# A new order of all engines for a two-branch cross-attention, with 9 score groups read from PSUM and 13 row by row

## The chip, the cores and the metric

The kernel runs on one core of a Trainium2 chip. A core has five engines with instruction queues of their own: TensorE (PE in the profile, with PEld for its weight loads), VectorE (DVE), ScalarE (ACT), GpSimd (POOL) and SyncE (SP), which here issues nearly all DMAs. The metric is the device time of one execution in microseconds. Before the change it was 500.68 us, the median of 3 runs (498.34 to 501.45).

## The reference

The inputs are tokens x (2 x 2048 x 640), a context (2 x 154 x 1024), six weight matrices and a bias, all float32. There are 20 heads of 32 channels. The first 77 context tokens are text, the other 77 an image prompt with key and value weights of its own; each half has its own softmax, and the two results are added.

```
q    = heads(x @ Wq.T)
k,v  = heads(text @ Wk.T), heads(text @ Wv.T)
k',v' = heads(ip @ Wk_ip.T), heads(ip @ Wv_ip.T)
out  = softmax(q k^T / sqrt(32)) v + softmax(q k'^T / sqrt(32)) v'
y    = merge_heads(out) @ Wo.T + bo + x
```

## The kernel before

All matrices lie with the contracted dimension first, so the 640 channels are five chunks of 128, and a chunk holds four heads. The work on one batch and one chunk is a pair; there are 10 pairs (batch 0 first). A pair's 2048 tokens are two units of 1024, so there are 20 units u = 0 to 19. A unit has two halves of 512 tokens (h) and three score groups (s) of 3, 3 and 2 blocks of 128 tokens; a group has 4 heads x 2 softmaxes for each block, so 24, 24 and 16 softmax rows of 77 keys on each partition.

The order of the whole program is written out by hand in `SCHEDULE` (from L560), a list of words that `emit` turns into instructions one after the other. Each engine executes its own instructions in that order; semaphores make it wait for data of the others. A word is a letter for the step, the unit or pair, and after the @ the PSUM bank or half of PSUM (8 banks, two halves of 4). The words that matter below:

- `q.u.h` the query product on TensorE (L199, five matmuls of 512 columns), `cq.u.h` its scaled copy out of PSUM on ScalarE (L209); `k.c.t` and `v.c.t` the key and value products (L140), `ck` and `cv` their copies.
- `Rs.u` the scores of group s on TensorE (L231: four heads side by side, 12 or 8 blocks in all). `Ks.u` copies them to the SBUF tile pb on ScalarE (L243), `Ms.u` takes the row maxima on VectorE (L279, or L282 from PSUM), `Ss.u` subtracts them on GpSimd (L293), `Es.u` is the exponential on ScalarE (one instruction, L299), `Ds.u` the row sums on VectorE (L304), `Is.u` their reciprocal (L309), `Ns.u` the normalising product on GpSimd (L314), `Ts.u` a transposition of 32 x 32 blocks on VectorE (L321).
- Three sets choose another way for a group (u, s). In DIRECT nothing is copied: the maxima and the exponentials read PSUM. In DIRECT and BIASED the exponential is one ScalarE instruction for each row, with the maximum as its bias (L267), and the subtraction on GpSimd falls away. In SUMMED, ScalarE adds up each row as well, and the sum on VectorE falls away. Groups of BIASED are first copied to SBUF.
- `A.q` the attention product of pair q on TensorE (L330: 80 matmuls in 32 x 32 tiles, 320 instructions with the weight loads), `CA.q` its copy out of PSUM. `SQ.c` and `VS.p.half` bring the values into the layout that it needs: a transposition on VectorE (L150), then eight small DMAs on SyncE (L156) for each VS.
- `LX.u.h` loads a block of 512 tokens of batch 1 (1280 KB, L184), `LQ.p` query weights (320 KB, L190), `LK.n` key or value weights (512 KB, L130), `LO` the output weights (1600 KB, L162, into the room of the context). `SF.i.part` fetches tokens to which the output is added (256 KB, L459 and L457), `SS.i.part` stores finished output (L465, L463). All of these stand in SyncE's one queue. The DMAs take eight semaphores in turn, so SyncE waits for an earlier DMA on the same semaphore before it issues the next on it.
- `m1` to `m7` with `.i` are the seven products of a Strassen-like scheme for the output projection of batch 0 (L488, L498), `cm` adds them to the output on VectorE (L513, L519); m3 joins the bank of m5 and so waits for cm5, as m6, m7 and m4 follow m1, m6 and m7. `G` and `W` are sums on GpSimd for it, `o` and `co` its last chunk (L469, L479). The output projection of batch 1 is a similar scheme with 33 products: `V` and `X` form sums of weights and tokens on VectorE (ending d) or GpSimd (ending p) at L826 and L832, `F` are the products (L846), `Y` the additions (L790, L792), each followed by a store (L796) once a block is finished.

[...] Outside the set-up all engine work is placed by the words above; nothing is placed by a scheduler.

Of the kernel before, what the change touches and what calls it, by code (L numbers as in the profile page):

```python
# [9 lines left out]
F32 = mybir.dt.float32  # L10
# [10 lines left out]
def kernel(  # L21
# [43 lines left out]
        (11, 0), (12, 0), (13, 0), (13, 2), (14, 0), (14, 2), (15, 1), (15, 2), (16, 2), (18, 1),  # L65
    }
    BIASED = {
        (3, 2), (4, 0), (5, 2), (6, 2), (8, 2), (9, 2), (10, 2), (11, 2), (12, 2), (18, 2), (19, 2),
    }
    SUMMED = {  # L70
        (10, 2), (12, 0), (12, 2), (13, 0), (13, 2), (14, 0), (15, 1), (16, 2), (18, 1), (18, 2), (19, 2),
# [480 lines left out]
    for t in range(2):  # L552
# [216 lines left out]
    for c, stages in enumerate(chains_of):  # L769
        for _, text in stages:  # L770
            for _, t in terms(text):
                for h in range(NH):
                    o = int(t[0]), NH * int(t[1]) + h
# [115 lines left out]
```

## Time and profile before

| | |
|---|---|
| median of 3 runs | 500.68 us (498.34 to 501.45) |
| profiled execution | 503.08 us, its span 501.3 us |
| TensorE busy | 492.2 us, 4114 passes |
| TensorE weight loads busy | 290.7 us, 4114 |
| VectorE busy | 410.7 us |
| ScalarE busy | 306.8 us |
| GpSimd busy | 376.5 us |
| granted TensorE clock over the span | 0.997 |
| DMA | 69.38 MB, mean 138 GB/s |

A page of the profile has the busy time of each engine, the span in 40 equal slices, the chain of work that ended last, and groups of instructions by line: operation, what is written from what, count, then busy time, mean of one in ns, and the idle time before them with what ended it. A row of the waits says which engine and line waited for whom: us in total, times, longest. A row of the timeline has start and duration in us, and in brackets the idle time before it. A row of the windows has the stretch, its length, then busy time and number of instructions of PE, PEld, DVE, ACT and POOL, then the granted TensorE clock, the DMA share and GB/s. In a row of the DMA view stand a queue, its packets, MB, and the share of the DMA engines' time; the queue of kind "instruction" numbered 8 brings TensorE's own program in packets of 16 KB. "Issue" is idle time in which an engine waited for nothing that the profile shows.

### The profile page before, as it was taken

The numbers are of one execution on the slowest core, as the hardware profiler recorded it, in microseconds if no ns is written. First come the engines' busy times: TensorE is split into PE (matmuls) and PEld (weight loads), VectorE is DVE, ScalarE is ACT, GpSimd is POOL, SyncE is SP. The second block draws the span as 40 slices with busy tenths as digits, with TensorE's granted clock in tenths as the row PEclk, the third lists the DMA queues.
The fourth block names the chain that finished last, engine by engine and source line by source line (L and its number), as shares of the span: only waits on it lengthen the run. The fifth ranks groups of instructions, "written<-read, shape, count | busy, mean of one in ns | idle before, by whom it ended". The sixth has DMA issues, their size and how long they took to land.

```text
span 501.3 us, 10439 instructions
## 1 busy us (share of the span) xinstructions
PE 492.2 (98%) x4114; PEld 290.7 (58%) x4114; DVE 410.7 (82%) x409; ACT 306.8 (61%) x970; POOL 376.5 (75%) x166
## 2 busy tenths in 40 slices
PE   9999999999999989999999999999999999999997
PEld 5665757567557547446646655665655685444442
DVE  0069989989999986978996888678799889998875
ACT  1175768798786866757999877485677955100000
POOL 0079998779898895968876748665889889799850
PEclk9999999999999998999999999999999999999999
DMA  8975403243044490748416337628442203320125
GB/s 264 356 209 151 133 3 100 54 119 84 23 112 150 150 288 19 248 133 330 134 54 229 94 119 274 222 87 264 144 158 90 86 1 106 127 84 1 43 101 192
DMA packets 67473, 69.38 MB, mean 138 GB/s; under 512 B 5472, under 2 KB 47200, under 8 KB 67424
## 3 DMA queue, kind: packets, MB, share of 16 engines
q1 hardware_dynamic: 66704, 68.00, 43.0%
q8 instruction: 32, 0.52, 0.4%
q10 hardware_dynamic: 720, 0.72, 0.4%
q14 instruction: 17, 0.14, 0.1%
HBM read 54.94 MB, written 10.49 MB: 131 GB/s over the span
## 4 chain that ended last, share of the span: by engine, by line
PE 90%; DMA 6%; SPq 2%; issue 1%; DVE 0%; ACT 0%
PE bank L199 30%; PE bank L846 11%; PE bank L488 10%; PE bank L231 10%; PE bank L330 10%; PE bank L140 9%; PE bank L469 7%; PE bank L498 3%; DMA x<-in_x_dram 2%; DMA aT<-in_L_xattn_Wk_ip_dram 2%; DMA wq<-in_L_xattn_Wq_dram 1%; DMA wo_ct<-in_L_xattn_Wo_dram 1%; SPq L156 1%; SPq L532 1%; SPq L130 0%
## 5 line engine op out<-in xcount | busy, mean ns | idle before, releaser
L314 POOL TENSOR_TENSOR pb<-pb,rden 128x1848 f32<-128x1848 f32 (+1 forms) x60 | 176.0, 2942 | 39.2 <-DVE rden L309 35.1
L199 PE MATMUL bank<-x,wq 128*128 128x512 f32 x400 | 180.0, 600 | 0.1
L293 POOL TENSOR_TENSOR pb<-pb,mx 128x1848 f32<-128x1848 f32 (+1 forms) x39 | 121.7, 3129 | 60.4 <-DVE mx L279 55.3
L199 PEld LDWEIGHTS bank<-x,wq 128*128 128x128 f32 x400 | 74.5, 191 | 85.9 <-issue 82.3
L321 DVE STREAM_TRANSPOSE pb<-pb 128x1920 f32<-128x1920 f32 (+1 forms) x60 | 115.8, 1934 | 6.3 <-POOL pb L314 5.9
L279 DVE TENSOR_REDUCE mx<-pb 128x24 f32<-128x1848 f32 (+1 forms) x50 | 91.4, 1843 | 31.6 <-ACT pb L243 31.5
L243 ACT COPY pb<-bank 128x462 f32<-128x462 f32 (+1 forms) x200 | 85.3, 540 | 42.2 <-PE bank L231 41.8
L304 DVE TENSOR_REDUCE den<-pb 128x24 f32<-128x1848 f32 (+1 forms) x49 | 91.5, 1878 | 15.6 <-ACT pb L299 11.9
L299 ACT ACTIVATE pb<-pb 128x1848 f32<-128x1848 f32 (+1 forms) x39 | 65.4, 1680 | 17.2 <-POOL pb L293 17.0
L267 ACT ACTIVATE pb<-bank,mx 128x77 f32<-128x77 f32 x208 | 59.1, 390 | 12.3 <-DVE mx L282 12.2
L231 PEld LDWEIGHTS bank<-kT,qT 32*128 32x128 f32 x1280 | 45.8, 184 | 29.7 <-issue 20.3
L231 PE MATMUL bank<-kT,qT 32*128 32x154 f32 x1280 | 57.0, 306 | 3.3 <-issue 2.6
L330 PE MATMUL bank<-pb,v 32*32 32x512 f32 x1600 | 55.2, 597 | 0.0
L267 ACT ACTIVATE pb<-pb,mx 128x77 f32<-128x77 f32 x184 | 52.7, 357 | 1.1 <-DVE mx L279 0.8
L140 PE MATMUL bank<-wo_ct,aT 128*128 128x154 f32 x320 | 46.9, 302 | 0.2 <-DMA aT<-in_L_xattn_Wk_ip_dram 0.2
L140 PEld LDWEIGHTS bank<-wo_ct,aT 128*128 128x128 f32 x320 | 44.4, 194 | 3.4 <-issue 2.8
L330 PEld LDWEIGHTS bank<-pb,v 32*32 32x32 f32 x1600 | 30.4, 103 | 21.7 <-issue 9.6
L267 ACT ACTIVATION_READ_ACCUMULATOR pb<-bank,mx 128x1 f32 x152 | 40.2, 273 | 0.0
L469 PE MATMUL bank<-aT,wo_ct 128*128 128x512 f32 x80 | 36.4, 596 | 0.0
L209 ACT ACTIVATE qT<-bank 128x512 f32<-128x512 f32 x40 | 24.3, 613 | 19.4 <-PE bank L199 19.3
L488 PE MATMUL bank<-aT,wo_ct 128*128 128x256 f32 x128 | 32.5, 386 | 0.6 <-DMA wo_ct<-in_L_xattn_Wo_dram 0.6
L488 PEld LDWEIGHTS bank<-aT,wo_ct 128*128 128x128 f32 x128 | 23.6, 190 | 8.3 <-issue 4.0
(75 smaller groups left out, 435.8 us busy)
## 6 DMA issues: line engine op xcount, KB each, us to landing
x<-in_x_dram SPq DMA_DIRECT2D x20, 1280.0 KB, 7.1
out_dram<-acc SPq DMA_DIRECT2D x20, 256.0 KB, 2.3
x<-in_x_dram SPq DMA_DIRECT2D x18, 256.0 KB, 5.4
acc<-in_x_dram SPq DMA_DIRECT2D x16, 256.0 KB, 3.7
out_dram<-x SPq DMA_DIRECT2D x15, 256.0 KB, 2.1
v<-vS SPq DMA_DIRECT2D x160, 20.0 KB, 2.0
wq<-in_L_xattn_Wq_dram SPq DMA_DIRECT2D x9, 320.0 KB, 4.7
aT<-in_L_xattn_Wk_dram SPq DMA_DIRECT2D x5, 512.0 KB, 5.6
```

The costliest lines, as they stand in the source:

```text
L140: nc.tensor.matmul(keys_in(out), loaded[n][:, k, :], cT[:, k, :, t, :], start=(k == 0), stop=(k == NCC - 1))
L199: nc.tensor.matmul(pq, wqs[q % 3][:, k, :], xs[place_of(u, h)][:, k, :], start=(k == 0), stop=(k == NC - 1),)
L231: nc.tensor.matmul(ps[g][:, ts(t, 2 * L)], qTs[(u, h)][g * D : (g + 1) * D, ts(st, P)], kT[g * D : (g + 1) * D, c, b].rearrange("p t l -> ...
L243: nc.scalar.copy(keys_of(u, s)[:, :, g], ps[g][:, : n * 2 * L].rearrange("p (n l) -> p n l", n=n))
L267: nc.scalar.activation(row, row if ps is None else rows_in(ps[g], n)[:, t, x], AF.Exp, bias=maxs[(u, s)][:, *one], accum_out=None if den i ...
L279: nc.vector.tensor_reduce(mx, rows_of(u, s), AX.X, ALU.max, negate=negate)
L293: nc.gpsimd.tensor_tensor(rows_of(u, s), rows_of(u, s), maxs[(u, s)].unsqueeze(3).to_broadcast([P, n, 2, L]), ALU.subtract)
L304: nc.vector.tensor_reduce(den_of(u, s), rows_of(u, s), AX.X, ALU.add)
L314: nc.gpsimd.tensor_tensor(rows_of(u, s), rows_of(u, s), rdens[(u, s)].unsqueeze(3).to_broadcast([P, n, 2, L]), ALU.mult)
L321: nc.vector.transpose(p, p)
L330: nc.tensor.matmul(pa[r][g * D : (g + 1) * D, :], v4s[q % 2][rows, g, k, :], zones[rows, :, g, k, :], start=(k == 0), stop=(k == NK - 1),)
L488: nc.tensor.matmul(part, w_of[m][:, kp, op], t_of(m, b, i)[:, kp], start=(op == kp == 0 and m in (1, 2, 5)), stop=(op == 1 and kp == 1 and ...
```

## The change

The same steps are written in a new order, on all engines: loads and stores of SyncE, the row-wise steps, the banks that products take, and which of the `V` and `X` sums run on VectorE or on GpSimd. In the new order each packet of TensorE's instructions was planned to arrive later by every large load that is under way when the packet is requested. No product is added or taken away, and TensorE's matmuls are the same in number and form.

Three sets change with it. DIRECT has 9 groups instead of 10, BIASED 13 instead of 11, SUMMED 13 instead of 11. GpSimd's sums become 151 instead of 160, VectorE's reductions 134 instead of 139, its sums of two tensors 86 instead of 78, ScalarE's activations 486 instead of 471 and its copies 286 instead of 282. Each line number of the kernel below the sets moves by 2.

```diff
     DIRECT = {
-        (11, 0), (12, 0), (13, 0), (13, 2), (14, 0), (14, 2), (15, 1), (15, 2), (16, 2), (18, 1),
+        (11, 0), (13, 0), (13, 2), (14, 0), (14, 2), (15, 1), (15, 2), (16, 2), (18, 1),
     }
     BIASED = {
-        (3, 2), (4, 0), (5, 2), (6, 2), (8, 2), (9, 2), (10, 2), (11, 2), (12, 2), (18, 2), (19, 2),
+        (2, 2), (3, 2), (4, 2), (5, 2), (6, 2), (7, 2), (9, 2), (11, 2), (12, 0), (12, 2), (18, 2), (19, 0),
+        (19, 2),
     }
     SUMMED = {
-        (10, 2), (12, 0), (12, 2), (13, 0), (13, 2), (14, 0), (15, 1), (16, 2), (18, 1), (18, 2), (19, 2),
+        (4, 2), (6, 2), (11, 2), (12, 0), (12, 2), (13, 0), (13, 2), (14, 0), (15, 1), (15, 2), (18, 1),
+        (18, 2), (19, 2),
     }
...
     SCHEDULE = (
...
-        "q.8.0@0 I2.5 T0.5 N2.5 K0.6 VS.2.1 I1.5 T2.5 N1.5 M0.6 R1.6@1 v.3.0@2 K1.6 M2.6 S0.6 LK.15 SF.0.3 E2.6 "
-        "M1.6 q.7.1@3 LK.16 T1.5 S1.6 E0.6 D2.6 A.2@1 I2.6 cv.3.0 D0.6 cq.7.1 N2.6 E1.6 I0.6 cq.8.0 T2.6 N0.6 D1.6 "
-        "R0.7@0 CA.2 k.4.1@4 I1.6 T0.6 K0.7 N1.6 v.3.1@5 ck.4.1 M0.7 R2.7@0 LK.19 cv.3.1 T1.6 R1.7@1 LX.10.0 S0.7 "
-        "K2.7 k.4.0@0 K1.7 M2.7 q.8.1@3 M1.7 E0.7 S2.7 ck.4.0 SQ.3 VS.3.1 S1.7 E2.7 D0.7 q.9.0@7 D2.7 E1.7 I2.7 "
-        "I0.7 N2.7 cq.8.1 SF.0.0 D1.7 LX.11.1 R2.8@0 N0.7 cq.9.0 VS.3.0 R0.8@1 K2.8 T2.7 q.9.1@0 K0.8 I1.7 M2.8 "
-        "N1.7 T0.7 E2.8 M0.8 R1.8@1 LX.11.0 q.10.0@1 LQ.7 LK.18 T1.7 K1.8 S0.8 cq.9.1 M1.8 E0.8 A.3@1 LX.10.1 D2.8 "
...
+        "T2.5 q.8.0@2 E2.6 N1.5 M0.6 LK.15 SF.0.3 T0.5 R1.6@1 S0.6 LX.10.0 LK.18 T1.5 q.7.1@1 K1.6 M1.6 E0.6 cq.8.0 "
+        "D0.6 S1.6 A.2@1 cv.3.0 cq.7.1 I2.6 I0.6 N0.6 E1.6 D1.6 R0.7@0 CA.2 v.3.1@4 I1.6 T0.6 K0.7 N1.6 k.4.1@5 "
+        "cv.3.1 M0.7 R2.7@0 ck.4.1 T1.6 R1.7@1 S0.7 K2.7 q.8.1@0 K1.7 M2.7 N2.6 M1.7 E0.7 E2.7 k.4.0@7 SQ.3 S1.7 "
+        "VS.3.0 D0.7 q.9.0@6 T2.6 E1.7 I0.7 D2.7 N0.7 LX.11.1 cq.8.1 I2.7 D1.7 ck.4.0 VS.3.1 R2.8@0 cq.9.0 R0.8@1 "
+        "K2.8 N2.7 T0.7 q.9.1@0 K0.8 I1.7 T2.7 N1.7 M2.8 R1.8@1 M0.8 LX.11.0 LK.19 S2.8 q.10.0@3 K1.8 SF.0.2 T1.7 "
+        "S0.8 E2.8 M1.8 cq.9.1 A.3@1 cq.10.0 D2.8 S1.8 E0.8 D0.8 E1.8 I0.8 I2.8 N0.8 R0.9@0 VS.5.0 CA.3 D1.8 "
...
-        "cq.10.1 I1.9 T2.9 R2.10@0 K0.10 N1.9 q.12.0@4 T0.9 K2.10 VS.5.1 T1.9 R1.10@0 cq.12.0 M0.10 A.4@1 K1.10 LO "
+        "q.12.0@4 LO T0.9 LQ.7 K2.10 VS.5.1 G5.0 T1.9 R1.10@0 cq.12.0 M0.10 A.4@1 K1.10 M2.10 S0.10 M1.10 S2.10 "
...
-        "I1.11 M0.12 N1.11 cq.13.0 E0.12 D2.11 G7.0 cm3.0 m6.0 I2.11 T1.11 N2.11 q.14.0@7 T2.11 M2.12 I0.12 E2.12 "
-        "M1.12 A.5@0 LX.14.1 N0.12 SF.1.4 LX.15.1 VS.6.1 S1.12 T0.12 m2.1@4 cm6.0 CA.5 I2.12 N2.12 E1.12 R0.13@0 "
+        "q.14.0@5 G6.0 LQ.8 I1.11 E2.12 T2.11 N1.11 M0.12 q.13.1@7 T1.11 E0.12 I2.12 M1.12 N2.12 A.5@0 LQ.9 LX.14.1 "
+        "G7.0 T2.12 S1.12 cm3.0 cm1.0 SS.0.0 LX.15.1 m6.0 I0.12 CA.5 N0.12 m2.1@4 cm6.0 SF.1.0 E1.12 VS.7.1 R0.13@0 "
...
-        "q.15.0@7 LX.17.1 SS.1.4 SS.0.2 T1.13 S1.14 SS.1.0 cm5.1 A.6@0 I0.14 cq.15.0 N0.14 E1.14 D1.14 I1.14 T0.14 "
-        "N1.14 o.2@7 CA.6 SF.2.0 SF.1.2 cq.15.1 LX.17.0 SF.2.4 G6.1 T1.14 SS.0.3 G4.1 R0.15@0 m3.1 K0.15 M0.15 "
+        "q.15.0@1 T1.13 S1.14 LX.17.1 SS.1.4 I0.14 cm1.1 A.6@1 cq.15.0 N0.14 E1.14 D1.14 I1.14 T0.14 N1.14 o.2@1 "
+        "CA.6 SF.2.4 SF.1.2 SS.1.0 SF.1.3 cq.15.1 LX.17.0 G6.1 T1.14 G7.1 R0.15@1 cm5.1 G4.1 SF.2.0 m3.1 K0.15 G5.2 "
...
-        "q.19.0@7 K0.18 D2.17 cq.18.1 I2.17 E1.17 I0.17 SS.2.0 N2.17 M0.18 R2.18@0 SF.3.0 N0.17 T2.17 m7.2 SF.2.3 "
+        "cm6.2 M1.17 S2.17 E0.17 D0.17 S1.17 E2.17 R0.18@0 SS.2.2 q.19.0@7 K0.18 SS.2.4 D2.17 LX.19.1 SF.3.0 I2.17 "
+        "M0.18 E1.17 N2.17 cq.18.1 D1.17 R2.18@0 S0.18 m7.2 K2.18 T2.17 R1.18@0 I1.17 E0.18 N1.17 o.3@5 M1.18 E1.18 "
...
```

101 rows, old and new, of the table SCHEDULE are left out of this document.

## The prediction

> **What bounds the kernel now.** I read the page's totals first, then TensorE's waits, then the clock by windows.
>
> ```profile
> span 501.3 us, 10439 instructions
> PE 492.2 (98%) x4114; PEld 290.7 (58%) x4114; DVE 410.7 (82%) x409; ACT 306.8 (61%) x970; POOL 376.5 (75%) x166
> ```
> ```profile
> PE bank L231 <- issue: 2.6, 2, 2.4
> ```
> ```profile
> PEclk9999999999999998999999999999999999999999
> ```
> ```profile
> 187.40:190.80 3.40, 3.40 (x19) 3.26 (x14) 2.21 (x3) 1.84 (x4) 3.03 (x2) 0.50 0.12 28
> ```
>
> TensorE (PE) is busy for 492.2 of 501.3 us, and the change leaves its 4114 passes as they are, so no order can win more than some 9 us. The longest of TensorE's few waits is 2.6 us of "issue" in two pieces: no data was late. The granted clock dips in one of the page's 40 slices alone; in the window of 187.4 to 190.8, right behind the larger piece, it stands behind the counts: 0.50 for 3.4 us, which costs 3.4 x 0.5 = 1.7 us more. I read the "issue" pieces as late instruction packets:
>
> ```profile
> q8 instruction: 32, 0.52, 0.4%
> ```
> ```profile
> 187.03:270.15 83.12, 82.12 (x762) 49.19 (x761) 67.52 (x62) 66.06 (x235) 65.58 (x28) 0.98 0.50 169
> ```
> ```profile
> 172.80 1.07 PE L231 MATMUL bank<-kT,qT 32*128 32x154 f32 x24
> 173.80 4.56 PE L199 MATMUL bank<-x,wq 128*128 128x512 f32 x10
> 178.29 5.52 PE L330 MATMUL bank<-pb,v 32*32 32x512 f32 x160
> 183.74 0.92 PE L231 MATMUL bank<-kT,qT 32*128 32x154 f32 x17
> 187.03 0.58 PE L231 MATMUL bank<-kT,qT 32*128 32x154 f32 x7 [2.38 <-issue]
> ...
> 260.81 5.52 PE L330 MATMUL bank<-pb,v 32*32 32x512 f32 x160
> ...
> 270.16 0.54 PE L231 MATMUL bank<-kT,qT 32*128 32x154 f32 x7 [0.20 <-issue]
> ```
>
> 32 packets for 8228 passes and weight loads are 257 instructions each. Between the two stalls stand 762 + 761 instructions and, by the order, 13 waits of the sequencer: 1536, six packets of 256 exactly. Both stalls come behind an attention product, in the middle of a score group (17 passes of 24, then 7): attention A.3 at 178.29 runs through 320 instructions in 5.5 us, more than a packet, so the next one is wanted shortly after it is asked for. Elsewhere a packet lasts 10 to 20 us. What held it back:
>
> ```profile
> 166.30 0.58 SPq L459 DMA_DIRECT2D acc<-in_x_dram  x1
> 166.98 0.41 SPq L184 DMA_DIRECT2D x<-in_x_dram  x1
> ...
> 174.57 0.53 SPq L184 DMA_DIRECT2D x<-in_x_dram  x1
> 175.20 0.47 SPq L190 DMA_DIRECT2D wq<-in_L_xattn_Wq_dram  x1
> 175.72 0.52 SPq L130 DMA_DIRECT2D aT<-in_L_xattn_Wv_dram  x1
> 178.39 0.98 SPq L184 DMA_DIRECT2D x<-in_x_dram  x1
> ```
> ```profile
> L184 SPq DMA_DIRECT2D x<-in_x_dram x1: 530/530/530, 174.6 to 174.6; - x1
> ...
> DMA to landing us min/median/max: 6.1/6.1/6.1
> ```
> ```profile
> L190 SPq DMA_DIRECT2D wq<-in_L_xattn_Wq_dram x1: 470/470/470, 175.2 to 175.2; - x1
> ...
> DMA to landing us min/median/max: 6.6/6.6/6.6
> ```
> ```profile
> L130 SPq DMA_DIRECT2D aT<-in_L_xattn_Wv_dram x1: 517/517/517, 175.7 to 175.7; - x1
> ...
> DMA to landing us min/median/max: 7.8/7.8/7.8
> ```
> ```profile
> q8 instruction: 1, 0.02, 68.6%
> ...
> q8 instruction: 1, 0.02, 69.3%
> ```
>
> The last fence holds one line each of the DMA views of 184.4 to 184.5 and of 267.72 to 267.80, in which the two packets start. The token load of 174.57 had landed at 180.7, the query weights of 175.20 at 181.8, the weights of 175.72 at 183.5. So the packet came 0.9 us behind the last load issued well before A.3, and ahead of the rest of the load of 178.39. From its start to the first instruction it took 187.03 - 184.4 = 2.6 us. A.3's **deadline** is thus 184.66 - 2.6 = 182.0, or 3.7 us after A.3 starts; it was missed by 2.4. A.5's packet starts at 267.7, 6.9 us after A.5 does, and is 0.2 too late.
>
> [...]
>
> **The change, part by part.** All is set against the profiled execution, 503.08 us (span 501.3 and 1.8 around it), 2.4 above the median of 500.68; I carry the difference over.
>
> *Loads around A.3.* Ahead of A.3, SyncE now issues the pieces VS.3.0, LX.11.1, VS.3.1, LX.11.0, LK.19 and SF.0.2; before it was VS.3.1, SF.0.0, LX.11.1, VS.3.0, LX.11.0, LQ.7, LK.18 and, at A.3 itself, LX.10.1. SF.0.0's issue is gone from in front (166.98 - 166.30 = 0.68 us), so LX.11.0 goes out at 3.7 + 0.7 = 4.4 us ahead of A.3 and lands 1.7 after A.3's start (6.1 us). LK.19, of the size of LK.18, lands 183.5 - 181.8 = 1.7 to 1.8 us behind what is in front of it (wq came 1.1 behind the token load), so at 3.5; SF.0.2, a fifth of a token load, near 4.3. The packet is expected between 0.4 us ahead of the last landing (A.5's case) and 0.9 behind, at 3.9 to 5.2, against 3.7. If SF.0.2 doesn't hold it, 3.1 to 4.4. The stall of **2.38 becomes 0 to 1.5; I take 0.8**. The half clock (**1.70**) I count as gone: the 0.65 us gap at 226.3 left no such window. A short gap that still closes the clock would cost the 1.70 again, and stays in the range.
>
> [...]
>
> *The output weights.*
>
> ```profile
> 204.36 15.37 SPq L156 DMA_DIRECT2D v<-vS  x16
> 219.77 0.59 SPq L162 DMA_DIRECT2D wo_ct<-in_L_xattn_Wo_dram  x1
> ...
> 226.95 1.13 PE L488 MATMUL bank<-aT,wo_ct 128*128 128x256 f32 x4 [0.65 <-DMA wo_ct<-in_L_xattn_Wo_dram]
> ```
>
> Before, LO stood behind 16 value spreads, 15.4 us of SyncE. Now it stands ahead of the last eight (VS.5.1), some 5 us earlier, while product m2.0 is in its old place: **0.65 goes.**
>
> *Loads around A.2 and A.5.* LX.10.0 and LK.18 now stand ahead of A.2. LX.10.0 waits for query product q.8.0, behind which TensorE still has a score group and q.7.1 (1.0 + 4.5 = 5.5 us, by the starts of 172.80, 173.80 and 178.29) before A.2; so it lands 0.6 after A.2's start, LK.18 at 2.4, the packet at 2.0 to 3.3, or 0.3 later if SyncE is slow to issue. Counted back 768 instructions, A.2's packet is wanted 0.6 us into the scores behind it: deadline 5.5 + 0.3 - 2.6 = 3.2. **Stall 0 to 0.5, taken 0.2.** At A.5, LQ.9 and LX.14.1 go out as it starts, and m6.0 comes in between it and the first instruction of its packet (eight passes of which four took 1.13 us at 226.95, the last one's tail included; some 1.8 us): deadline near 6.7 + 1.8 = 8.5. LX.14.1 goes out 0.5 after A.5's start and lands some 7 us later behind LQ.9, near 7.4; the packet is due at 7.0 to 8.3. **The 0.20 goes; 0 to 0.4 in its place, taken 0.1.** The other attentions have no token load issued in the 6 us before them, or want their packet much later.
>
> *New waits of the engines.*
>
> ```profile
> 306.29 5.52 PE L330 MATMUL bank<-pb,v 32*32 32x512 f32 x160
> ...
> 317.23 1.13 PE L488 MATMUL bank<-aT,x 128*128 128x256 f32 x4
> ```
> ```profile
> L314 POOL TENSOR_TENSOR pb<-pb,rden 128x1848 f32<-128x1848 f32 x40 | 131.2, 3287 | 26.9 <-DVE rden L309 23.4 <-ACT pb L267 2.2 <-ACT pb L243 1.0
> ...
> L304 DVE TENSOR_REDUCE den<-pb 128x24 f32<-128x1848 f32 x35 | 72.1, 2063 | 13.6 <-ACT pb L299 11.9 <-ACT pb L267 1.6
> ...
> L299 ACT ACTIVATE pb<-pb 128x1848 f32<-128x1848 f32 x33 | 58.0, 1761 | 16.3 <-POOL pb L293 16.2
> ...
> L209 ACT ACTIVATE qT<-bank 128x512 f32<-128x512 f32 x40 | 24.3, 613 | 19.4 <-PE bank L199 19.3
> ...
> L513 DVE SCALAR_TENSOR_TENSOR acc<-bank,bo_sb,acc 128x256 f32<-128x256 f32 x32 | 13.6, 466 | 5.0 <-PE bank L498 5.0
> ...
> L321 DVE STREAM_TRANSPOSE pb<-pb 128x1920 f32<-128x1920 f32 x40 | 86.0, 2154 | 4.8 <-POOL pb L314 4.7
> ```
>
> cm5.1, which frees the bank for m3.1, moves on VectorE from ahead of A.6 to behind D1.14, I1.14, T0.14 and T1.14. From A.6's start the chain is the query copy 0.61, exponential 1.76, sum 2.06, normalising 3.29, transpose 2.15 and cm5.1's two halves 0.93: 10.8, and a reciprocal and the hand-overs come on top. TensorE's cover, A.6 to the product, is 317.23 - 306.29 = 10.9. Wait 0 to 0.7, taken 0.4. Likewise cq.18.1, which R2.18 needs, falls behind E1.17 on ScalarE, which waits for POOL's S1.17: 0 to 1.76 (E1.17's length), taken 0.4. **Together 0.8.**
>
> *Where groups are read.* (12,0) is copied out instead of being read from PSUM; (2,2), (4,2), (7,2), (12,0), (19,0) join the row-by-row groups, (4,0), (8,2), (10,2) leave them; four join those summed on ScalarE and two leave.
>
> ```profile
> L267 ACT ACTIVATE pb<-pb,mx 128x77 f32<-128x77 f32 x184 | 52.7, 357 | 1.1 <-DVE mx L279 0.8
> ```
>
> A 16-row group costs ScalarE 16 x 0.36 = 5.7 us instead of one exponential. With 40 such rows more, 24 fewer from PSUM and 32 more row sums ScalarE's work grows by 9 to 15 us and POOL's shrinks by some 10; eight sums of V and X move from POOL to VectorE. By the busy shares at the top each of the three has 90 us idle or more, so I cost all this at nothing beyond the two waits above. Where a bank were held longer it would show as a wait of L231 for ScalarE.
>
> **Sum:** -2.38 - 1.70 - 0.65 - 0.20 = -4.93; +0.8 + 0.2 + 0.1 + 0.8 = +1.9; together -3.0. Profiled 503.08 - 3.0 = 500.1, median **497.7**.
>
> **The rivals.**
> 1. *Full gain.* No packet is late and the engines' waits hide: -4.9 to -5.4 with hand-overs, 495.3 to 496.7. For it: every new lateness has zero as an end. Against: three attentions within 1 us of their deadline.
> 2. *The loads are not the cause*, or the runs without a profile have no such stall (they spread over 3.1 us). Then A.3 stalls as before or nothing was lost there: -0.85 + 0.8, 500.6. For it: 16 KB is little beside the 1280 of a token load, and it did overtake the rest of the load of 178.39. Against: the packet starting 0.9 us behind a landing in one case and beside one in the other.
> 3. *Slower.* A.2's and A.3's packets both come 2.4 us past the deadline, each closing the clock: 2 x 4.08 + 0.8 - 4.93 = +4.0, 504.7. It decides at A.2: there the packet must start later than 5.5 us after the attention, 3.1 behind LK.18's landing, which neither observed packet did.
>
> **How the numbers follow.** Forecast (496.7 to 499) 0.45, full gain 0.2, rival 2 with milder lateness (499 to 501.5) 0.2, slower 0.1, something unseen 0.05. Range: low end full gain, 495.3; high end A.3 at 1.5 us with the clock closed and all waits at their upper values, 5.7 to 6 against 4.93, near 501.5; about 2 in 10 lie outside. One per cent, about what a measurement of this kernel can tell, is 5 us: faster by more 0.08, within 0.85, slower by more 0.07.
>
> **What would show it.** Right: TensorE's "issue" wait under 1.5 us in all, no half-clock window behind 20 us, no wait of L490 (the old L488) for wo_ct, one wait of a product for VectorE near 310. Wrong: a gap of 2 us behind A.2, A.3 or A.5; a half-clock window; waits of the scores for ScalarE's row-by-row exponentials of over 1 us.

## The result and the profile after

The kernel after takes **497.87 us** (median of 9 executions, 497.00 to 498.50), beside 500.94 us of the kernel before in 9 (498.34 to 502.32): a ratio of **0.9941, 95% interval 0.9922 to 0.9961**. A second set of executions gave 497.65 us in 12 and 0.9946 (0.9925 to 0.9967). The forecast was 497.7. Its sum came out for partly wrong reasons, as the experiments show. One execution among the experiments took 1844 us, slow from end to end, and is left out of its median.

The profiled execution of after took 498.50 us. These are the lines of its page that answer to those of before:

```profile
span 496.7 us, 10482 instructions
PE 490.3 (99%) x4114; PEld 287.9 (58%) x4114; DVE 408.5 (82%) x412; ACT 315.0 (63%) x1021; POOL 362.5 (73%) x157
PEclk9999999999999999999999999999999999999999
q8 instruction: 32, 0.52, 0.5%
```

The span is 4.6 us shorter. TensorE's busy time fell by 1.9 us (492.2 to 490.3), nearly all of it the half clock of 1.70, and its idle time by 2.7 (9.1 to 6.4). All of TensorE's waits of after (who, for what: us in total, times, longest), and the window of time in which the clock had been halved before:

```profile
PE bank L549 <- DVE pb L547: 1.1, 1, 1.1
PE bank L201 <- DMA x<-in_x_dram: 0.5, 1, 0.5
PE bank L233 <- ACT kT L559: 0.3, 1, 0.3
PE bank L142 <- DMA aT<-in_L_xattn_Wk_ip_dram: 0.3, 1, 0.3
PE bank L490 <- DVE acc L515: 0.2, 1, 0.2
```
```profile
187.40:190.80 3.40, 3.40 (x47) 3.24 (x50) 3.40 (x2) 1.93 (x6) 3.19 (x1) 1.00 0.11 24
```

No "issue" and no wo_ct is left, and the granted clock of that window is 1.00. The first four waits belong to the set-up, of which the 0.5 for x is new; the one new wait in the body is that of product m3.1 for VectorE. A wait of before that the prediction doesn't list, of scores for a copy of the keys at 57 us, is gone too:

```profile
PE bank L231 <- ACT kT L684: 0.4, 1, 0.4
```

With these the waits and the half clock account for the 4.6 us to 0.1: -2.38 - 0.20 - 1.70 - 0.65 - 0.4 is -5.3, and 0.5 + 0.2 + 0.1 (the wait for weights in the set-up grew) is +0.8. The timeline around A.3 shows TensorE without a gap, then SyncE's queue, then the line of the DMA view of 182.50 to 182.60, in which the packet of instructions starts:

```profile
178.95 5.52 PE L332 MATMUL bank<-pb,v 32*32 32x512 f32 x160
184.40 1.07 PE L233 MATMUL bank<-kT,qT 32*128 32x154 f32 x24
185.40 0.79 PE L142 MATMUL bank<-wo_ct,aT 128*128 128x154 f32 x4
```
```profile
174.64 0.53 SPq L186 DMA_DIRECT2D x<-in_x_dram  x1
175.21 0.52 SPq L132 DMA_DIRECT2D aT<-in_L_xattn_Wv_ip_dram  x1
175.78 0.79 SPq L461 DMA_DIRECT2D acc<-in_x_dram  x1
183.46 6.05 SPq L158 DMA_DIRECT2D v<-vS  x8
```
```profile
q8 instruction: 1, 0.02, 71.1%
```

The packet starts 3.6 us after A.3 does, a moment before the landing of LK.19 (182.7) and 0.8 us before that of SF.0.2 (183.3). Its first instruction, behind some 17 of the 24 score passes, is due 2.5 us later. By the deadline that the prediction worked out, 3.7 us after A.3 starts, it came just in time.

### The profile page after: what moved, and what is told of

It reads as the page before. It is cut to its first block, busy times and chain, and to the rows that moved or that the text cites. A ratio compares the mean times of both kernels' runs of the same rounds, so it can differ in the third digit from the quotient of the medians.

```text
span 496.7 us, 10482 instructions
## 1 busy us (share of the span) xinstructions
PE 490.3 (99%) x4114; PEld 287.9 (58%) x4114; DVE 408.5 (82%) x412; ACT 315.0 (63%) x1021; POOL 362.5 (73%) x157
## 4 chain that ended last, share of the span: by engine, by line
PE 92%; DMA 3%; SPq 1%; DVE 1%; POOL 1%; ACT 1%; issue 0%; POOLq 0%
PE bank L201 33%; PE bank L848 11%; PE bank L490 10%; PE bank L233 10%; PE bank L332 10%; PE bank L142 9%; PE bank L471 6%; PE bank L500 3%; DMA aT<-in_L_xattn_Wk_ip_dram 2%; DMA wq<-in_L_xattn_Wq_dram 2%; SPq L534 1%; POOL pb L316 1%; DVE den L306 0%; ACT pb L301 0%; SPq L132 0%
## 5 line engine op out<-in xcount | busy, mean ns | idle before, releaser
L295 POOL TENSOR_TENSOR pb<-pb,mx 128x1848 f32<-128x1848 f32 (+1 forms) x38 | 119.3, 3152 | 51.8 <-DVE mx L281 51.5
L281 DVE TENSOR_REDUCE mx<-pb 128x24 f32<-128x1848 f32 (+1 forms) x51 | 93.7, 1850 | 30.7 <-ACT pb L245 30.5
L245 ACT COPY pb<-bank 128x462 f32<-128x462 f32 (+1 forms) x204 | 87.2, 539 | 36.0 <-PE bank L233 35.4
L306 DVE TENSOR_REDUCE den<-pb 128x24 f32<-128x1848 f32 (+1 forms) x47 | 88.7, 1895 | 17.6 <-ACT pb L301 13.3
L301 ACT ACTIVATE pb<-pb 128x1848 f32<-128x1848 f32 (+1 forms) x38 | 64.2, 1696 | 17.8 <-POOL pb L295 17.5
L269 ACT ACTIVATE pb<-pb,mx 128x77 f32<-128x77 f32 x224 | 67.8, 364 | 0.3 <-DVE mx L281 0.2
L269 ACT ACTIVATE pb<-bank,mx 128x77 f32<-128x77 f32 x184 | 51.8, 386 | 9.3 <-DVE mx L284 9.3
L142 PE MATMUL bank<-wo_ct,aT 128*128 128x154 f32 x320 | 45.6, 296 | 0.3 <-DMA aT<-in_L_xattn_Wk_ip_dram 0.3
L142 PEld LDWEIGHTS bank<-wo_ct,aT 128*128 128x128 f32 x320 | 42.9, 188 | 3.6 <-issue 2.2
L269 ACT ACTIVATION_READ_ACCUMULATOR pb<-bank,mx 128x1 f32 x128 | 33.6, 267 | 0.0
```

The source lines that it names most:

```text
L142: nc.tensor.matmul(keys_in(out), loaded[n][:, k, :], cT[:, k, :, t, :], start=(k == 0), stop=(k == NCC - 1))
L245: nc.scalar.copy(keys_of(u, s)[:, :, g], ps[g][:, : n * 2 * L].rearrange("p (n l) -> p n l", n=n))
L269: nc.scalar.activation(row, row if ps is None else rows_in(ps[g], n)[:, t, x], AF.Exp, bias=maxs[(u, s)][:, *one], accum_out=None if den i ...
L281: nc.vector.tensor_reduce(mx, rows_of(u, s), AX.X, ALU.max, negate=negate)
L295: nc.gpsimd.tensor_tensor(rows_of(u, s), rows_of(u, s), maxs[(u, s)].unsqueeze(3).to_broadcast([P, n, 2, L]), ALU.subtract)
L306: nc.vector.tensor_reduce(den_of(u, s), rows_of(u, s), AX.X, ALU.add)
```

## The experiments

The theory: SyncE's large loads that are under way when a packet is asked for hold it back, the late packet stalls TensorE behind A.3, and the stall can halve the clock. The rivals: the loads are not the cause; the stall is there in profiled executions alone; the gain comes from the rest of the new order. Each matmul of the program stands in the traces as two passes and two weight loads (the seven of the warm-up are 14 passes), so four of TensorE's instructions. In each diff of loads below stand SyncE's words from LK.19 or A.2 on, in their order.

**Two loads moved, in the kernel before**

```diff
-LK.19 LX.10.0 VS.3.1 SF.0.0 LX.11.1 VS.3.0 LX.11.0 LQ.7 LK.18 A.3@1 LX.10.1 VS.5.0
+LK.19 LK.18 LX.10.0 VS.3.1 SF.0.0 LX.11.1 VS.3.0 LX.11.0 A.3@1 LX.10.1 LQ.7 VS.5.0
```

> The kernel before with two loads alone moved away from attention A.3: LK.18 to right behind LK.19, LQ.7 to behind LX.10.1. Nothing else differs. Theory (large loads under way hold the instruction packet back): the last load that is wholly ahead of A.3 is then LX.11.0, which landed at 180.7, so the packet starts near 180.7 to 181.6 instead of 184.4, inside its deadline of 182.0; the issue wait of 2.38 us and the half clock of 1.70 behind it go, 4.1 us of the profiled execution and about as much of the median: 496.9. A.5's 0.20 and the 0.65 for wo_ct stay. Rival (the loads are not the cause): the gap of 2.4 us and the half-clock window stay, the median within 0.5 us of the kernel before. Second rival (the stall is there in profiled executions alone): the gap goes from the profile, the median does not move.

500.61 us, beside 500.26 of the kernel before on that chip: a ratio of 0.9988 (0.9964 to 1.0013), so no gain where 496.9 was expected. The timeline of its TensorE, and of its SyncE:

```profile
179.29 5.52 PE L330 MATMUL bank<-pb,v 32*32 32x512 f32 x160
184.75 0.92 PE L231 MATMUL bank<-kT,qT 32*128 32x154 f32 x17
186.87 0.54 PE L231 MATMUL bank<-kT,qT 32*128 32x154 f32 x7 [1.21 <-issue]
```
```profile
175.07 4.70 SPq L184 DMA_DIRECT2D x<-in_x_dram  x2
179.82 0.52 SPq L190 DMA_DIRECT2D wq<-in_L_xattn_Wq_dram  x1
```

A gap of 1.21 us is left. The packet started at 184.4, not behind LX.11.0 (landed 181.1) but inside the next token load: LX.10.1 went out at 179.4, 0.1 us after A.3's start, and landed at 186.5. It was under way 5.0 us before the packet started; no view shows when a packet is requested. The expectation had left that load out. The clock was 1.000 in the profile, yet 0.997 or less in 4 of the 12 executions.

**Three loads moved.** LX.10.1 now waits until A.3 is over.

```diff
-LK.19 LX.10.0 VS.3.1 SF.0.0 LX.11.1 VS.3.0 LX.11.0 LQ.7 LK.18 A.3@1 LX.10.1 VS.5.0
+LK.19 LK.18 LX.10.0 VS.3.1 SF.0.0 LX.11.1 VS.3.0 LX.11.0 A.3@1 VS.5.0 LX.10.1 LQ.7
```

> The kernel before with three loads moved away from A.3: LK.18 to behind LK.19, and LX.10.1 and LQ.7 to behind VS.5.0, which goes out once A.3 is over. Against the run with two loads moved it differs in LX.10.1 (and LQ.7 behind it), which there went out 0.1 us after A.3's start; its packet started 5.1 us after A.3 did and left a gap of 1.2 us. Theory (any large load issued ahead of the packet's request, about 1 us into the attention, holds it): now LX.11.0 is the last such load, landing 1.8 us after A.3's start, and the packet starts by 3.7 us after it, so no gap over 0.3 us behind A.3; no clock under 0.998 in more than 1 of 12 runs; median 498.1 to 498.9, being the 499.3 of the open-clock runs of the two-load version less 1.2, with some room for the start of the kernel. Rival (the packet is slow there whatever is loaded): a gap of 1 us or more stays, 0.997 or less in 3 or 4 of 12 runs, median 500 to 500.7.

498.55 us (11 executions), 0.9962 of the kernel before (0.9941 to 0.9982). Its profile comes from one more execution.

> One look at the kernel before with three loads moved away from A.3, for its profile, since the profiled execution of the timed run was a disturbed one throughout (1844 us). Theory: A.3's packet starts within 3.7 us of A.3's start and TensorE has no issue wait over 0.3 us behind A.3; A.5's of 0.2 us stays; time 497.4 to 499.4 as in the other eleven runs. Rival (the packet is slow there in any order of the loads): a gap of 1 us or more.

497.36 us. TensorE's timeline:

```profile
177.97 5.52 PE L330 MATMUL bank<-pb,v 32*32 32x512 f32 x160
183.42 1.07 PE L231 MATMUL bank<-kT,qT 32*128 32x154 f32 x24
184.42 1.85 PE L140 MATMUL bank<-wo_ct,aT 128*128 128x154 f32 x12
```

The gap is gone. The packet started at 180.1, 2.1 us after A.3 and 1.6 ahead of the deadline of 3.7. LX.11.0 landed just then (180.2), but that doesn't show that it held the packet: in the trace of before, the packets behind A.0 and A.1 start at 71.33 and 108.42, 2.2 us after the attentions (69.13 and 106.21), and no large load is under way when they do. So the packet was as early here as those two, and in before, at 6.1 us after A.3, it came some 4 later. The 1 us that the expectation sets between the start of A.3 and the packet's request is an estimate of the author's that no run shows. In no execution was the clock under 0.999. So three words of the loads take the gap away.

**Two loads put back, in the kernel after**

```diff
-LX.10.0 LK.18 A.2@1 VS.3.0 LX.11.1 VS.3.1 LX.11.0 LK.19 SF.0.2 A.3@1 VS.5.0 LX.10.1
+LX.10.0 A.2@1 VS.3.0 LX.11.1 VS.3.1 LX.11.0 LQ.7 LK.18 LK.19 SF.0.2 A.3@1 VS.5.0 LX.10.1
```

> The kernel after with two loads put back ahead of A.3 as they were before: LQ.7 and LK.18 behind LX.11.0, ahead of LK.19. Nothing else differs. Theory: the query weights took 1.1 us and the K/V weights 1.75 us of landing time in the trace of before, so A.3's packet starts some 2.8 us later than the 182.5 of after, at 185.4; its first instruction, just in time in after, is 2.8 us late. TensorE shows an issue wait of 2.5 to 3 us behind A.3; with the clock closing behind it, 1.7 more: median 500.5 to 502.5. Rival (the loads are not the cause): no issue wait, median 497.9 within 0.5.

499.57 us, level with before (0.9991, 0.9968 to 1.0014), and this gap:

```profile
177.81 5.52 PE L332 MATMUL bank<-pb,v 32*32 32x512 f32 x160
183.26 1.05 PE L233 MATMUL bank<-kT,qT 32*128 32x154 f32 x18
185.57 0.54 PE L233 MATMUL bank<-kT,qT 32*128 32x154 f32 x6 [1.27 <-issue]
```

The direction is the theory's, the size half of what was expected: the packet started 5.1 us after A.3 instead of 3.6, between the landings of LK.18 (181.7) and LK.19 (183.6) and not behind all of them. The clock was 0.997 in 3 of 12.

**All three put back, in the kernel after**

```diff
-LX.10.0 LK.18 A.2@1 VS.3.0 LX.11.1 VS.3.1 LX.11.0 LK.19 SF.0.2 A.3@1 VS.5.0 LX.10.1
+LX.10.0 A.2@1 VS.3.0 LX.11.1 VS.3.1 LX.11.0 LQ.7 LK.18 LK.19 SF.0.2 A.3@1 LX.10.1 VS.5.0
```

> The kernel after with the loads around A.3 as before: LQ.7 and LK.18 behind LX.11.0, and LX.10.1 at A.3's start. Against the version with two loads put back (gap 1.27 us, 0.997 in 3 of 12 runs, 499.4 to 499.6) it adds LX.10.1. Theory: a gap of 1.3 to 2.5 us behind A.3, clock of 0.997 or less in 3 to 6 of 12 runs, median 499.5 to 500.6: most of what the whole change won is given back by these three words. Rival (what the change won lies elsewhere): 497.9 to 498.6, no issue wait.

500.98 us, 1.0007 of the kernel before (0.9980 to 1.0034): the whole gain is given back. So three words of the loads also bring the gap back. It is no longer than with two loads, but in this profiled execution the clock closed behind it (windows of time: length, busy time of PE, PEld, DVE, ACT and POOL, granted clock, DMA share, GB/s):

```profile
186.00 0.54 PE L233 MATMUL bank<-kT,qT 32*128 32x154 f32 x6 [1.32 <-issue]
```
```profile
183.65:187.06 3.41, 2.09 (x32) 1.69 (x29) 2.84 (x3) 3.41 (x12) 3.41 (x2) 1.00 1.05 368
187.06:190.47 3.41, 3.41 (x16) 3.41 (x14) 3.41 (x2) 0.87 (x3) 2.75 (x1) 0.50 0.43 132
190.47:193.88 3.41, 3.41 (x56) 3.25 (x55) 0.84 (x3) 1.08 (x4) 3.06 (x1) 1.00 0.03 6
```

The clock was 0.997 or less in 6 of the 12. These have a median of 501.6, the other six one of 499.7, against 497.65 of after. Of these 2.1 us the gap of the trace is 1.3; the rest is not shown.

**The packets shifted, no load moved, in the kernel before**

```diff
-    for _ in range(7):
-        nc.tensor.matmul(banks[0][:, :P], warm, warm, start=True, stop=True)
+    for _ in range(2):
+        nc.tensor.matmul(banks[0][:, :448], warm[:, :P], warm[:, :448], start=True, stop=True)
```

> The kernel before with its seven warm-up matmuls of 128 columns replaced by two of 448: as many columns, 20 instructions of TensorE fewer. No load is moved. Every packet of 256 instructions then begins 20 instructions later in the program: A.3's on the third pass of v.4.0 instead of 7 passes before the end of the scores R0.9, and A.5's likewise beyond its score group. Theory (a packet wanted too early): the deadline of A.3's packet is later by those 7 passes of 0.04 us and by 3 of v.4.0's of 0.14, 0.7 us, and the packet still starts at about 184.4, so a gap of 1.7 us is left, now on the line of v.4.0 instead of the scores; with a gap that short the clock may stay open, which would take 0.7 to 2.4 us off the median. A.5's 0.20 goes. Rival (the gap belongs to the scores, whatever the packet): 2.4 us on the scores' line as before, and no change.

499.01 us, 0.9982 (0.9963 to 1.0002): by that interval not told apart from before. TensorE's timeline:

```profile
184.00 1.07 PE L231 MATMUL bank<-kT,qT 32*128 32x154 f32 x24
186.46 1.95 PE L140 MATMUL bank<-wo_ct,aT 128*128 128x154 f32 x13 [1.38 <-ACT aT L357]
```

The scores now run without a break, 24 of 24, and the gap, 1.38 us, stands ahead of v.4.0 (of its first pass, where the third was expected) and ends 2.5 us after the packet's start (183.97). The profile puts the wait down to ScalarE's copies of A.3, the last of which ended just then; but in the run with three loads moved v.4.0 began 1.0 us after the first of the same copies, and in the run of four loads and the same warm-up, further down, it did so too. So the gap follows the packet through the program. The stall behind A.5 is gone. The clock was 0.997 or less in 1 of 12.

**The packets shifted the other way, in the kernel after**

```diff
-    for _ in range(7):
-        nc.tensor.matmul(banks[0][:, :P], warm, warm, start=True, stop=True)
+    for _ in range(15):
+        nc.tensor.matmul(banks[0][:, :60], warm[:, :P], warm[:, :60], start=True, stop=True)
```

> The kernel after with fifteen warm-up matmuls of 60 columns instead of seven of 128: as many columns, 32 instructions of TensorE more. No load is moved. Every packet begins 32 instructions earlier in the program. Theory: A.3's packet, just in time in after, is wanted 16 score passes of 0.04 us earlier: a gap of 0.6 us behind A.3; the packet behind A.6 is wanted right behind the attention instead of in the product m3.1: a gap of 0.6 to 1.6 us there; the other packets have 0.9 us or more to spare. Together 1.2 to 2.2 us on the median, 499.1 to 500.1, if gaps that short leave the clock open; if they close it, 1.7 more for each. Rival (no packet is late by itself, the gap of before came from its loads or its order alone): no issue wait and 497.9.

502.14 us, later than expected. Most of that is a cost of the edit itself: the columns were as many, but a pass of 60 columns took about as long as one of 128 (30 passes in 6.65 us, 14 in 3.35), and the first scores began at 26.4 instead of 23.6 (the second profile of after). Some 1.0 us of the 4.5 above after's 497.65 is not accounted for by this and the gap below. Of the two gaps only one came:

```profile
303.13 5.50 PE L332 MATMUL bank<-pb,v 32*32 32x512 f32 x159
309.30 0.58 PE L332 MATMUL bank<-pb,v 32*32 32x512 f32 x1 [0.67 <-issue]
```

A packet that begins at the last pass of A.6 is late by 0.67 us. At A.3 the packet started 2.6 us after the attention instead of 3.6, and was in time. No execution had a clock under 0.999: 0.67 us didn't close it.

**The output weights put back, in the kernel after**

```diff
-LX.12.1 LO LQ.7 VS.5.1 A.4@1
+LX.12.1 LQ.7 VS.5.1 A.4@1 LO
```

> The kernel after with LO put back behind VS.5.1 and A.4, its place before. It would be issued near 217.4 instead of 205.9 (VS.5.1's eight spreads take 10.9 us of SyncE there), and land some 7 us later, 224.5, while product m2.0 is due at 222.5. Theory (the wait of 0.65 went because LO was moved): TensorE waits 0.65 to 2.0 us for wo_ct at L490, median 498.5 to 499.9. Rival (m2.0 has other cover, or LO lands as fast as it can behind smaller loads): a wait under 0.3 us, median 497.9 within 0.4.

497.80 us, level with after, and no wait for wo_ct. SyncE reached LO at 213.5, not at 217.4, since its eight spreads took 7.1 us here; LO landed at 220.6, 0.9 ahead of m2.0. With LO in its old place the traces show waits of 0.65, none, 0.70, 0.27 and none (before, two loads moved, packets shifted, three loads moved, this one).

**Four loads and the warm-up, in the kernel before.** LK.18, LX.10.1 and LQ.7 as in the run with three loads moved; the two warm-up matmuls of 448 columns; and LO:

```diff
-VS.5.1 A.4@1 LO
+LO VS.5.1 A.4@1
```

> The kernel before with four loads moved (LK.18 behind LK.19, LX.10.1 and LQ.7 behind VS.5.0, LO ahead of VS.5.1) and two warm-up matmuls of 448 columns in place of seven of 128. Sets, row-wise steps, banks, products and everything else are as before. Theory (the change wins by the place of these loads and by nothing else): no wait for wo_ct, no issue wait over 0.2, clock of 0.998 or more in at least 11 of 12 runs, median 497.4 to 498.2, level with the kernel after (497.65 to 497.9) and below the 498.55 of three loads moved. Rival (the new order of the row-wise steps and the sets is worth something by itself): 498.4 or more.

**497.76 us**, 0.9948 (0.9928 to 0.9967), level with after. Sets, row-wise steps and banks are those of before. Its trace has no issue wait and none for wo_ct; it has one of 0.70 us of a product at L488 for VectorE, which the trace of before doesn't have.

**The bank freed early, in the kernel after.** The two warm-up matmuls of 448 columns, and:

```diff
-cm1.1 A.6@1
+cm1.1 cm5.1 A.6@1
...
-R0.15@1 cm5.1 G4.1
+R0.15@1 G4.1
```

> The kernel after with cm5.1 ahead of A.6, as it was before, and two warm-up matmuls of 448 columns in place of seven of 128. Theory: the wait of m3.1 for VectorE (0.24 us at L490) goes, and A.3's packet has 0.8 us more to spare; nothing else is late, so 497.3 to 497.6, 0.1 to 0.4 below the kernel after. Rival: cm5.1 in its old place delays the softmax of head pair 6 and the 0.24 comes back as another wait, or the warm-up costs its later start (0.9 us): 497.7 to 498.6.

497.59 us (7 executions), 0.9937 (0.9913 to 0.9961). The wait of m3.1 is gone from the trace; the time is the same within its scatter (497.65 to 497.87 for after). 0.24 us can't be told apart here.

**The row-by-row sets of before, but for (12,0), in the order of after**

```diff
     BIASED = {
-        (2, 2), (3, 2), (4, 2), (5, 2), (6, 2), (7, 2), (9, 2), (11, 2), (12, 0), (12, 2), (18, 2), (19, 0),
-        (19, 2),
+        (3, 2), (4, 0), (5, 2), (6, 2), (8, 2), (9, 2), (10, 2), (11, 2), (12, 0), (12, 2), (18, 2), (19, 2),
     }
...
-E2.4
+S2.4 ... E2.4 D2.4
```

> The kernel after with the row-by-row sets of before, but for group (12,0): (2,2), (4,2), (7,2), (19,0) are subtracted by GpSimd again, (4,0), (8,2), (10,2) are not; (4,2), (6,2), (11,2), (15,2) are summed by VectorE again, (10,2), (16,2) are not. The new steps stand right behind the step that feeds them; the rest of the order is as after. Theory (which groups go row by row is off the path): no new wait of TensorE over 0.3 us, median within 0.5 of 497.65. Rival (the sets carry part of the gain, GpSimd's 10 us less being needed): a wait of the scores or of an attention for GpSimd or ScalarE of 1 us or more, 498.6 or more.

525.89 us, 28 us more. The first five of TensorE's waits:

```profile
PE bank L488 <- DVE acc L519: 3.8, 1, 3.8
PE bank L330 <- DVE pb L321: 2.9, 2, 1.6
PE bank L330 <- issue: 2.8, 2, 2.0
PE bank L488 <- DVE acc L513: 2.6, 2, 2.4
PE bank L231 <- ACT kT L684: 2.1, 1, 2.1
```

The clock closed in four stretches of its profile, at 1.7 us each. The earliest gap, 0.81 us ahead of A.1 at 106.4, can be followed. GpSimd now subtracts group (4,2), for 2.25 us from 96.3; its exponential comes behind that, VectorE stands idle for 1.55 us at the sum D2.4 that I put right behind it, and the transposes T2.3 and T1.3, which A.1 needs, are queued behind the sum. This run doesn't tell the sets from the places that I gave their steps, so it settles nothing on the sets by themselves. It shows that sets and order belong together: few spare microseconds lie between an engine's neighbouring steps, for all its 90 us of idle time. That the old sets in their old order cost nothing is shown by the run of four loads and the warm-up.

| kernel | median us | gap behind A.3 in its profile | executions with clock 0.997 or less |
|---|---|---|---|
| before, beside the experiments | 500.10 | 2.38 | 23 of 84 |
| before, two loads moved | 500.61 | 1.21 | 4 of 12 |
| before, three loads moved | 498.52 | 0 | 0 of 12 |
| before, packets shifted | 499.01 | 1.38 | 1 of 12 |
| before, four loads and warm-up | 497.76 | 0 | 0 of 9 |
| after, both sets | 497.81 | 0 | 0 of 21 |
| after, two loads back | 499.57 | 1.27 | 3 of 12 |
| after, three loads back | 500.98 | 1.32 | 6 of 12 |

## Why the prediction was right, and where it was wrong

- **The mechanism held.** The stall behind A.3 is a late instruction packet, and large loads hold it: moving three loads in before takes it away (2.38 us in the profile of before, none with the three moved), putting them back in after brings it back (none, then 1.32), and shifting the program by 20 instructions moves the gap to another line (1.38 ahead of v.4.0).
- **How a load holds a packet was told too simply.** "0.9 us behind the last landing" was too strict a rule: with two loads back the packet started between two landings, and LX.10.1, issued as A.3 begins, counts too. Nor does every large load under way hold a packet, as the plan of the new order takes it. Behind A.2 in after, LX.10.0 and LK.18 landed 2.5 and 4.0 us after the attention's start, and the packet began at 2.2, no later than behind A.0 of before, where no such load was under way; in the second profile of after they landed at 3.6 and 5.2, and it began at 2.1; in the profile with LO put back they landed at 2.5 and 4.1, and it began at 3.1. The runs show which loads matter at A.3, not what decides when a load holds a packet: that stays open.
- **The step "2.38 becomes 0.8" was mis-sized at both ends.** After has no gap: its packet came at 3.6, in the branch where SF.0.2 doesn't hold it (3.1 to 4.4), not at 3.9 to 5.2. And 2.38 was the gap of one execution: executions of before with an open clock have a median of 499.71 (61 of them), with three loads moved 498.52, 1.2 less, and the gaps in the profiles with two loads moved, with two and three back and with the packets shifted are 1.2 to 1.4. That the ordinary gap of before is 1.2 is worked out from these times; no trace shows such an execution.
- **The step "half clock 1.70, counted as gone" took a chance for a certainty.** Of 84 executions of before, 23 had a clock of 0.997 or less, with a median of 502.20; the profiled one (503.08, 0.997) was of that kind. On the median the closed clock is worth 500.10 - 499.71 = 0.4 us, not 1.70. The doubt stood in the prediction, as the second half of rival 2, and should have gone into the sum.
- **"0.65 goes"**: it went, but the move of LO isn't shown to be the reason. With LO behind the spreads it went as well, in the one profile of that run: SyncE got to it at 213.5 there and at 219.8 in before, and it landed 7.1 later in both.
- **A.5's 0.20 went**, and nothing came in its place (0.1 taken): the packet started 5.2 us after A.5, where 7.0 to 8.3 was foreseen. **A.2: nothing** (0.2 taken); its deadline was set 0.3 too early, since the sum adds 0.3 where the text counts 0.6 us into the scores, and nothing hung on it. **R2.18: nothing** (0.4 taken).
- **m3.1 for VectorE: 0.24 us** where 0.4 was taken, on the chain that was foreseen, query copy to cm5.1:

```profile
311.10 1.07 PE L233 MATMUL bank<-kT,qT 32*128 32x154 f32 x24
312.41 1.13 PE L490 MATMUL bank<-aT,x 128*128 128x256 f32 x4 [0.24 <-DVE acc L515]
```

- **The sets at nothing**: right for this change, since before reaches the same time with the old ones. The sizes foreseen were a little off: ScalarE's busy time rose by 8.2 us (9 to 15), GpSimd's fell by 14.0 (some 10). The reason given, 90 us of idle time, was not a good one: the old sets, put into the new order with their steps where I placed them, cost 28 us.
- **The sum.** Between the profiled executions it was to be -3.0 and was -4.6: rival 1, the full gain, is what the two profiles show. Between the medians it was to be -3.0 and was -3.07, or -2.3 over all executions (500.10 to 497.81). The 1.7 us of new lateness that didn't come (1.9 taken, 0.24 measured) made up for a stall and a half clock that ordinary executions have only in part. That the medians agree to 0.2 us is luck in this sense: the late packet was the right mechanism, but the losses of before and the new lateness were both taken too large, and the two errors cancel. And one per cent is not the limit of what can be told of this kernel: the interval of the first comparison is 0.2% wide to either side.

## What to carry to other kernels

Before a loss that one profile shows goes into a sum, see whether the other executions have it: the clock of each told here that 23 of 84 had one of 0.997 or less. Where a gap like the one behind A.3 (320 instructions in 5.5 us, the next packet starting 6.1 us after the first) stands in a trace, look at the loads issued shortly before and as these instructions start, and move them to see which matter; here four words of the load order and the number of warm-up matmuls, in an otherwise unchanged schedule, were worth the whole change. An engine's idle share doesn't say what a step may cost in a fixed order (90 us idle here, and the sets put back cost 28); its neighbours do.

## What the runs showed of the hardware

The granted clock was halved for 3.41 us at a time: in before (187.40 to 190.81), with three loads back (187.06 to 190.47) and four times with the sets put back, where the starts (149.58, 176.88, 245.15 and 344.14) lie 8, 20 and 29 times 3.413 us apart. In before the first clock record begins at 6.50 us, and the 180.91 us from it to the closing are 53 times that. Two stretches ahead of a closing and two others with a stall, from the run with the sets put back (two rows for each, the stretch and the next):

```profile
146.17:149.58 3.41, 1.46 (x43) 0.82 (x50) 3.41 (x2) 2.06 (x2) 1.32 (x1) 1.00 0.85 281
149.58:152.99 3.41, 3.41 (x67) 2.04 (x60) 2.90 (x4) 0.85 (x3) 2.75 (x1) 0.50 0.05 12
221.26:224.67 3.41, 2.11 (x68) 1.10 (x68) 3.41 (x3) 1.89 (x4) 0.39 (x2) 1.00 1.03 401
224.67:228.08 3.41, 3.41 (x111) 1.91 (x93) 3.04 (x2) 0.30 (x1) 3.37 (x2) 1.00 0.92 286
241.74:245.15 3.41, 1.94 (x36) 1.63 (x36) 3.41 (x6) 3.01 (x12) 0.63 (x1) 1.00 0.71 196
245.15:248.56 3.41, 3.41 (x10) 2.68 (x9) 3.38 (x4) 2.59 (x7) 3.41 (x2) 0.50 0.71 274
258.80:262.22 3.42, 1.94 (x9) 1.76 (x10) 3.42 (x5) 1.18 (x2) 1.84 (x1) 1.00 0.64 222
262.22:265.63 3.41, 3.41 (x33) 2.14 (x32) 3.41 (x5) 1.50 (x4) 2.09 (x2) 1.00 0.37 102
```

and from the runs with two loads back and with two loads moved, where no closing marks the stretches and their places are the author's estimate, counted on by that length from the first clock record (6.56 + 52 x 3.413; 3.92 + 53 x 3.413):

```profile
184.06:187.47 3.41, 2.14 (x20) 1.75 (x18) 3.15 (x3) 3.41 (x11) 3.41 (x2) 1.00 0.15 34
```
```profile
184.82:188.23 3.41, 2.20 (x30) 1.94 (x31) 3.34 (x2) 3.27 (x12) 3.41 (x2) 1.00 0.37 103
```

Stretches in which TensorE was busy for 1.46, 1.94 or 2.09 us (the last in the run with all three loads back) were followed by half clock; those with 2.11, 2.14, 2.20 and another of 1.94 were not; nor was one of 1.83 (337.30 to 340.72 in the run with the sets put back), so the busy time alone doesn't decide. Behind a gap of 1.32 us (three loads back) the clock was halved, behind one of 1.27 (two loads back) it was not, and of the four kernels with gaps of 1.21 to 1.38 us in their profiles one to six of twelve executions had a clock of 0.997 or less. What decides it is not shown. In the stretch ahead of that closing the idle time was 1.3 us, 3.41 less 2.09.
